# A graph attention layer: fetching 38 gathered rows a group by plain DMAs from two queues instead of 8 from one

## The chip, the cores and the metric

The kernel runs on one core of one Trainium2 chip. The metric is the device time of one execution in microseconds. Five engines work side by side: TensorE (PE, with its weight loads as PEld), VectorE (DVE), ScalarE (ACT), GpSimd (POOL) and SyncE (SP). Each has a queue of its own, worked off in order; semaphores tie them together.

## The reference

A graph has N = 12500 nodes and 212500 edges, sorted by destination. Node and edge features have 128 columns, in 8 heads of 16.

```python
Q = (x @ WQ).reshape(N, H, dh)
K = (x @ WK).reshape(N, H, dh)
V = (x @ WV).reshape(N, H, dh)
Eh = (edge_attr @ WE).reshape(-1, H, dh)
score = K[src] * Q[dst] / jnp.sqrt(jnp.float32(dh)) * Eh
score = jnp.exp(jnp.clip(score.sum(-1, keepdims=True), -5.0, 5.0))
msg = V[src] * score
wV = jax.ops.segment_sum(msg, dst, num_segments=N)
Z = jax.ops.segment_sum(score, dst, num_segments=N)
h = x + (wV / (Z + ATTN_EPS)).reshape(N, D)
# batch norm of h over the nodes, then layer norm of (x + that)
```

All data is float32. What this case is about is `K[src]` and `V[src]`: every edge needs the keys and values of its source node.

## The kernel before, in words

The edges stand in 1661 tiles of 128 edges, and up to 8 tiles make a group; there are 208 groups. First the kernel computes K and V of all nodes as one table `kvd` in DRAM, 1 KB a node (`table_rows`). For the first groups, while the table is still being made, it gathers x and projects it (`project_main`); from the ninth group on it gathers rows of the table into slots in SBUF, eight slots and one more later on.

The usual gather is one indirect DMA a tile, issued by POOL (line 223, `gather`): 128 rows of 1 KB by the node ids in `srcs`. The gathers of a group wait in a list, `queued`. In the main loop `pace` ties the first one of them to a matmul of the group (`add_x` or `q_mm`), and `issue` gives POOL the rest. A slot is free again when the message of its group has been computed.

Some tiles are gathered in another way. For each group in the list made by `row_plan`, the last of its eight tiles is not gathered by POOL. Its 128 rows are fetched one at a time by plain DMAs of 1 KB from SP (line 283, in `fetch_rows`), `SP_ROWS` = 8 of them in each group of the loop, into a tile `byrow` with two buffers. SP reads the byte offsets of the rows from `row_ids` into registers (line 276) and then issues a MOVE and a DMA a row. A tile so needs 16 groups of the loop to be filled, and it is used two groups after its last row (`ROW_LAG`). Twelve tiles are fetched so, 1536 rows. They count on semaphores of their own, `rows_in`; DVE waits for them (`rows_there`) before it uses such a tile, and it treats that tile apart from the other seven, in an instruction of its own, both for the product (line 630) and for the message (line 655).

The main loop is written out by hand, and each engine takes the instructions of a pass in that order. The parts that matter here are:

- SP loads `ea` for the group four ahead (line 508, three buffers), `relT` in fours (line 406) or singly (line 419), then fetches the rows.
- PE: `add_x` of the group three back (lines 696 and 697), `q_mm` of three ahead (563), `gather_sum` of the one before (670 and 671), `eh_mm` (584), `turn_back` (617), `qe_mm` (599).
- ACT: `x_out` of three back (701), `q_window` (525 and 532), `q_hi`, which copies Q out of PSUM (567), the two exponentials of this group in `clip_exp` (646 and 647), `sums_out` (676), the second copy of Q (572), `eh_out` (591).
- DVE: `products` (630), `q_lo` (575), `both_halves` (609), `scores` (637), the clip (645), `denom`, `recip` and `attn` (680, 683, 687), the one-hots (553, 543 to 546), `q_mid` (571), the message (655).

After the loop come the last groups, the two norms and the store of the output. A second way of computing it all, for inputs in another order, is not taken here.

Of the kernel before, what the change touches and what calls it, by code (L numbers as in the profile page):

```python
# [10 lines left out]
U8 = mybir.dt.uint8  # L11
I32 = mybir.dt.int32
AF = mybir.ActivationFunctionType
OP = mybir.AluOpType
AX = mybir.AxisListType
ET = mybir.EngineType

P = 128
# [4 lines left out]
U = 4  # L23
# [4 lines left out]
EARLY = 3  # L28
RUN = 64
ROWS = P  # L30
FIRST_ROW = 3
LATE = 8
ROW_LAG = 2
SP_ROWS = 8
WORDS = 4
RQ = 4
NSEM = 6
# [5 lines left out]
def plan(N, T):  # L43

    n, r = divmod(T - sum(LAST), U)
    sizes = [U] * n + [r] * (r > 0) + list(LAST)
    assert n > 1 and len(sizes) % 2 == 0
    starts = [sum(sizes[:g]) for g in range(len(sizes))]
    cuts = list(range(0, N - 64, CH)) + [N - 64, N]
    due = {}  # L50
    thr = [0.0] * len(sizes)
    for j, c in enumerate(cuts[1:]):
        need = (c + (64 if c < N - CH else 24)) * T
        g = next((g for g, t in enumerate(starts) if t * N >= need), None)
        if g is not None:
            due.setdefault(g, []).append(j)
            thr[g] = float(c)
    return sizes, starts, cuts, due, thr


def row_plan(sizes):


    full, n = sizes.count(U) // 2, SP_ROWS
    groups, end = [], P
    while FIRST_ROW + -(-end // n) - 1 + ROW_LAG < full:
        groups.append(max(NX, FIRST_ROW + -(-end // n) - 1 + ROW_LAG))
        end += P
    assert sorted(set(groups)) == groups
    return groups  # L70
# [7 lines left out]
def gnn_kernel(  # L78
# [19 lines left out]
    nc = tc.nc  # L98
    N, D = out.shape
    T = src.shape[1]  # L100
    NW = dstb.shape[1]
    usizes, ustarts, cuts, due, _ = plan(N, T)
    NG = NW // 2
    sizes = [usizes[2 * g] + usizes[2 * g + 1] for g in range(NG)]
# [5 lines left out]
    consts = ctx.enter_context(tc.tile_pool(name="consts", bufs=1))  # L110
# [50 lines left out]
    def load_rest():  # L161
        nc.scalar.dma_start(base_i, bass.AP(tensor=dstb.tensor, offset=dstb.offset, ap=[[0, P], [1, NW]]))
        nc.scalar.dma_start(rel_i[:, :cut], dst[:, :cut])
        load_row_ids()
        nc.scalar.dma_start(w_q, wq)
        nc.scalar.dma_start(w_e, we)
        nc.scalar.dma_start(srcs[:, nxg * G:cut], src[:, nxg * G:cut])

    def load_last():
        nc.scalar.dma_start(rel_i[:, cut:], dst[:, cut:])  # L170
        nc.scalar.dma_start(srcs[:, cut:], src[:, cut:])
        nc.scalar.dma_start(gb[:, 0:1], gamma)
        nc.scalar.dma_start(gb[:, 1:2], beta)
# [55 lines left out]
    def issue(n=0):  # L229
        while len(queued) > n:  # L230
            f, *a = queued.pop(0)
            f(*a)

    def pace(step):
        if queued:
            f, *a = queued.pop(0)
            tc.add_manual_dep(f(*a).ins, step.ins.name,
                              mybir.DependencyInfo(mybir.DependencyClass.Sync, mybir.DependencyReason.DATA),
                              reason="pace")
# [2 lines left out]

    by_row, fill = {}, {}
    row_loads = []
    n = SP_ROWS
    row_tiles = row_plan(usizes)
    tot = len(row_tiles) * P
    cols = -(-n // WORDS) * WORDS
    full_rows = tot // n
    blocks = -(-tot // (P * n))  # L250
    for q in range(0, full_rows, P):
        row_loads.append((0, q // P * cols, min(P, full_rows - q), n, q * n))
    if tot % n:
        row_loads.append((full_rows % P, full_rows // P * cols, 1, tot % n, full_rows * n))
    for q in range(-(-tot // n)):
        fill[FIRST_ROW + q] = q
    by_row.update({g: None for g in row_tiles})
    rows_in = [tc.alloc_semaphore(f"rows_in{i}") for i in range(NSEM)]
    row_ids = consts.tile([P, blocks * cols], I32, name="row_ids")
    nc.vector.memset(row_ids, 0)  # L260
    kvb = kvd.bitcast(U8).rearrange("n d -> (n d)")

# [1 line left out]
        return [(a, b - 1), (b - 1, b)] if g in by_row and b == G else [(a, b)]  # L264

    def load_row_ids():
        for p, c, m, w, at in row_loads:
            nc.scalar.dma_start(row_ids[p:p + m, c:c + w], bass.AP(
                tensor=rsrc.tensor, offset=rsrc.offset + at, ap=[[n, m], [1, w]]))

    def fetch_rows(g):
        if g not in fill:
            return
        q = fill[g]
        c = q // P * cols
        _, offs = nc.values_load_multi_w_load_instructions(
            row_ids[q % P:q % P + 1, c:c + cols], engines=(ET.SP,), min_val=0, max_val=(N - 1) * 8 * P,
            skip_runtime_bounds_check_because="node ids")
        for r, off in zip(range(q * n, min(q * n + n, tot)), offs):
            k = row_tiles[r // P]  # L280
            if r % P == 0:
                by_row[k] = rows.tile([P, 1, 2 * P], F32, name="byrow", bufs=2)
            d = nc.sync.dma_start(by_row[k][r % P:r % P + 1, 0, :].bitcast(U8), kvb[ds(off, 8 * P)].unsqueeze(0))
            d.then_inc(rows_in[r // P % NSEM], 16)
            tc.no_tile_sem_insts.add(d.ins.name)
            tc.add_to_no_dep_group(f"rows{k}", d.ins)
# [66 lines left out]
    def within(f, g):  # L353
        return f(g) if 0 <= g < NG else None
# [47 lines left out]
    def load_quad(q):  # L402
        t = late[0].tile([P, RQ, U * P], BF16, name="rbq", bufs=2)
        for h in (0, 1):
            at = ustarts[2 * RQ * q + h] * P
            nc.sync.dma_start(t[h * WN:(h + 1) * WN], bass.AP(
                tensor=relT.tensor, offset=relT.offset + at, ap=[[0, WN], [G * P, RQ], [1, U * P]]))
        for k in range(RQ):
            RB[RQ * q + k] = t[:, k, :]
# [191 lines left out]
    def ehqe(g):  # L601
        eh_mm(g)
        eh_out(g)
        qe_mm(g)
# [143 lines left out]
    for q in range(NQ):  # L748
# [13 lines left out]
        k = q - first_step  # L762
# [12 lines left out]
    q_mid(2)  # L775
    turn_back(0)
    ehqe(1)
    nc.vector.tensor_scalar(row_ids, row_ids, 8 * P, None, op0=OP.mult)
    within(load, 2)
    turned_onehot(2)  # L780
    load_rel(3)
# [10 lines left out]
    def bn_parts(a, b):  # L792
        for w in range(a, b):
            for j in due.get(w, []):
                bn_part(j)
                done.add(j)
# [22 lines left out]
    def within_checks(g):  # L819
        if g >= first_check and (g - first_check) % every == 0:  # L820
            check((g - first_check) // every)
# [6 lines left out]
    for g in range(NG - 2):  # L828
        within(load, g + 4)
        within(load_rel, g + 5)  # L830
        if (g + 6) % RQ == 0 and (g + 6) // RQ in quads:
            load_quad((g + 6) // RQ)
        fetch_rows(g)
        within(products, g)
        within(q_lo, g + 2)
        within(both_halves, g + 1)
        step = within(add_x, g - 3)
        step = within(q_mm, g + 3) or step
        if step is not None and queued and g >= LATE + 4:
            pace(step)  # L840
        issue()
        within(x_out, g - 3)
        within(q_window, g + 4)
        within(q_hi, g + 3)
        within(gather_sum, g - 1)
        within(eh_mm, g + 2)
        if g + 1 < nxg and g + 1 not in SLOT:
            for _ in project_main(g + 1):
                pass
        within(turn_back, g + 1)  # L850
        within(scores, g)
        within(clip_exp, g)
        within(sums_out, g - 1)
        within(denom, g - 2)
        within(recip, g - 2)
        within(attn, g - 2)
        within(turned_onehot, g + 3)
        within(onehot, g)
        within(q_mid, g + 3)
        within(eh_out, g + 2)  # L860
        within(qe_mm, g + 2)
        within(message, g)
        if g == NG - 3:
            onehot(g + 1)
        if g == 2:
            load_last()
        for r in runs[1:]:
            if g == max(4, r[0] // 2 - 12):
                place(r)
        within_checks(g)  # L870
        while free and todo and not pending:
            load_x()
        bn_parts(2 * g - 5, 2 * g - 3)
        if g == NG - 5:
            assert done >= set(range(NPRE))
            norm_first()
        if g == LATE - 1:
            tps.close()
            late.append(tps.enter_context(tc.tile_pool(name="late", bufs=1)))
        if g == LATE - 2:  # L880
            free.append(NSLOT)
            load_kv()
    last = NG - 1
    g = last - 1
# [4 lines left out]
                           skip_runtime_bounds_check_because="a count")]  # L889
# [7 lines left out]
    step = add_x(g - 3)  # L897
# [53 lines left out]
    pairs = [[i] for i in range(min(2, NY))] + [list(range(i, min(i + 2, NY))) for i in range(2, NY - 1, 2)]  # L951
# [261 lines left out]
```

## Time and profile before

| | |
|---|---|
| time, median of 3 runs | 2605.09 us (2600.39 to 2608.06) |
| the profiled execution | 2606.08 us, its span 2604.3 us |
| busy, share of the span | PE 72%, PEld 49%, DVE 64%, ACT 26%, POOL 61% |
| granted TensorE clock, mean | 0.839 |
| gathers by POOL (line 223) | 1585, mean 950 ns |
| row DMAs by SP (line 283) | 1536 of 1.0 KB |
| traffic | 148 GB/s over the span |

A line of a group in the profile gives the source line, the engine, the operation, what it writes and reads, the count, the busy time, the mean of one, and the engine's idle time just before it with what ended it. In a timeline the columns are the start in us from the start of the span, the length in us, the engine, the line, the operation, what it writes and reads and how many instructions were merged, with the idle time before it in brackets. The names SPq and ACTq stand for instructions that the engine's queue handles itself, among them the issue of DMAs; they are not counted as busy time. In a table by windows, the columns are the stretch, its length, the busy time of the engine with the number of instructions, the granted clock, the share of the DMA engines and GB/s.

### The profile page before, as it was taken

The numbers are of one execution on the slowest core, as the hardware profiler recorded it, in microseconds if no ns is written. First come the engines' busy times: TensorE is split into PE (matmuls) and PEld (weight loads), VectorE is DVE, ScalarE is ACT, GpSimd is POOL, SyncE is SP. The second block draws the span as 40 slices with busy tenths as digits, with TensorE's granted clock in tenths as the row PEclk, the third lists the DMA queues.
The fourth block names the chain that finished last, engine by engine and source line by source line (L and its number), as shares of the span: only waits on it lengthen the run. The fifth ranks groups of instructions, "written<-read, shape, count | busy, mean of one in ns | idle before, by whom it ended". The sixth has DMA issues, their size and how long they took to land. (4 is left out here: it accounts for less than half of the span.)

```text
span 2604.3 us, 34575 instructions
## 1 busy us (share of the span) xinstructions
PE 1872.5 (72%) x9414; PEld 1273.5 (49%) x9414; DVE 1656.1 (64%) x3577; ACT 677.8 (26%) x2480; POOL 1594.7 (61%) x1685
## 2 busy tenths in 40 slices
PE   7657677777777676777767767767776776677687
PEld 5435444444445454445545444445544454444456
DVE  3335666666666766666666666666666666666687
ACT  2223222222222222222222222222222222222235
POOL 6633566666666666666666666666666666666624
PEclk8978888888888988878787878888888888787889
DMA  7733454545445454454544544545445454454454
GB/s 231 245 110 97 143 149 141 155 145 149 147 139 157 146 149 145 138 157 138 157 145 140 149 142 148 147 146 146 149 142 150 142 152 145 141 155 138 144 161 118
DMA packets 175393, 386.62 MB, mean 148 GB/s; under 512 B 37518, under 2 KB 91831, under 8 KB 175191
## 3 DMA queue, kind: packets, MB, share of 16 engines
q0 software_dynamic: 78128, 212.05, 28.4%
q1 hardware_dynamic: 92900, 169.50, 20.7%
q10 hardware_dynamic: 4163, 2.78, 0.4%
q8 instruction: 77, 1.26, 0.2%
q14 instruction: 125, 1.02, 0.1%
HBM read 364.57 MB, written 19.63 MB: 148 GB/s over the span
## 5 line engine op out<-in xcount | busy, mean ns | idle before, releaser
L223 POOL DMA_INDIRECT slot<-kvd,srcs x1585 | 1506.0, 950 | 893.5 <-issue 416.9
L671 PE MATMUL ps_a<-msg,oh 128*128 128x136 f32 (+1 forms) x3322 | 705.8, 368 | 58.2 <-ACT os L676 48.3
L671 PEld LDWEIGHTS ps_a<-msg,oh 128*128 128x128 f32 (+1 forms) x3322 | 582.6, 222 | 170.7 <-issue 109.1
L609 DVE TENSOR_TENSOR wt<-wt,ps_q 128x512 f32<-128x512 f32 x416 | 276.5, 685 | 504.1 <-remote 212.1
L696 PE MATMUL ps_m<-ident,at 128*128 128x128 f32 x412 | 123.2, 390 | 492.6 <-issue 192.3
L584 PE MATMUL ps_e<-ea,w_e 128*128 128x512 f32 x832 | 395.2, 595 | 5.5 <-issue 4.9
L701 ACT ACTIVATE hx<-ps_m 128x64 f32 x412 | 93.2, 226 | 1137.6 <-PE ps_e L584 345.7
L696 PEld LDWEIGHTS ps_m<-ident,at 128*128 128x128 f32 x412 | 80.5, 243 | 585.5 <-issue 242.1
L630 DVE TENSOR_TENSOR p<-slot,ps_t 128x512 f32<-128x512 f32 (+1 forms) x410 | 264.0, 677 | 135.7 <-remote 91.7
L617 PEld LDWEIGHTS ps_t<-ident,wt 128*128 128x128 f32 x1661 | 191.8, 141 | 207.1 <-issue 142.4
L617 PE MATMUL ps_t<-ident,wt 128*128 128x128 f32 x1661 | 244.5, 278 | 64.9 <-issue 38.8
L591 ACT ACTIVATE wt<-ps_e 128x512 f32<-128x512 f32 x416 | 231.0, 587 | 128.7 <-remote 40.1
L637 DVE TENSOR_REDUCE s<-p 128x64 f32<-128x1024 f32 (+1 forms) x209 | 252.2, 1207 | 0.1
L655 DVE TENSOR_TENSOR msg<-slot,ps_m 128x1024 f32<-128x1024 f32 (+2 forms) x209 | 246.8, 1183 | 0.4 <-ACT ps_m L646 0.3
L543 DVE TENSOR_TENSOR oh<-ps_m,rel_i 128x512 f32<-128x512 f32 x208 | 142.3, 684 | 143.0 <-ACT ps_m L646 135.7
L584 PEld LDWEIGHTS ps_e<-ea,w_e 128*128 128x128 f32 x832 | 146.0, 194 | 109.2 <-issue 105.4
L599 PE MATMUL ps_q<-ot,q 64*128 64x512 bf16 x1248 | 174.6, 384 | 6.7 <-issue 6.7
L572 ACT ACTIVATE q<-qr 128x128 bf16<-128x128 f32 x208 | 64.7, 311 | 300.9 <-DVE qr L571 178.2
L563 PE MATMUL ps_m<-w_q,xw 128*128 128x128 f32 x416 | 109.4, 355 | 8.8 <-issue 8.6
L697 PE MATMUL ps_m<-xw,ident 128*128 128x128 f32 x412 | 106.7, 350 | 3.1 <-issue 2.9
L563 PEld LDWEIGHTS ps_m<-w_q,xw 128*128 128x128 f32 x416 | 89.9, 266 | 12.3 <-issue 12.2
L670 PE MATMUL ps_a<-os,carry 64*1 64x136 f32 x414 | 94.6, 314 | 1.2 <-issue 1.2
(173 smaller groups left out, 1516.3 us busy)
## 6 DMA issues: line engine op xcount, KB each, us to landing
ea<-eaT SPq DMA_DIRECT2D x207, 512.0 KB
slot<-kvd,srcs POOLq DMA_INDIRECT x1585
byrow<-kvd SPq DMA_DIRECT2D x1536, 1.0 KB
rbq<-relT SPq DMA_DIRECT2D x94, 256.0 KB
kvd<-slot SPq DMA_DIRECT2D x12, 512.0 KB
kvd<-t SPq DMA_DIRECT2D x12, 512.0 KB
slot<-xT SPq DMA_DIRECT2D x24, 256.0 KB
out<-o SPq DMA_DIRECT2D x23, 256.0 KB
```

The source lines that it names most:

```text
L223: return nc.gpsimd.indirect_dma_start(out=out, out_offset=None, in_=table, in_offset=bass.IndirectOffsetOnAxis(ap=srcs[:, e:e + 1], axis=0))
L563: return nc.tensor.matmul(PQ[g], XW[g], w_q, start=True, stop=True)
L584: nc.tensor.matmul(eh, w_e, EA[g][:, a:b, :].rearrange("p a b -> p (a b)"), start=True, stop=True)
L591: nc.scalar.activation(t[:, :(b - a) * P], EH[g][h], AF.Copy)
L599: nc.tensor.matmul(QE[g][h], Q3[g][r, k, :], OT[g][r, :(b - a) * P], start=(k == 0), stop=(k == 2))
L609: nc.vector.tensor_tensor(t, t, QE[g][h], op=OP.mult)
L617: nc.tensor.transpose(ps[:, j, :], WT[g][h][:, j * P:(j + 1) * P], ident)
L630: step = nc.vector.tensor_tensor(PR[g][:, c:d, :], KV[g](c, d, 0), PW[g][i][:, c - a:d - a, :], op=OP.mult)
L637: nc.vector.tensor_reduce(SS[g][:, a:b, :], PR[g][:, a:b, :].rearrange("p t (h d) -> p t h d", d=DH), axis=AX.X, op=OP.add)
L655: step = nc.vector.tensor_tensor(MSG[g][:, a:b, :P].rearrange("p t (h d) -> p t h d", d=DH), KV[g](a, b, P).rearrange("p t (h d) -> p t h ...
L671: nc.tensor.matmul(AGG[g][WN if j >= n else 0:], OH[g][j], MSG[g][:, j, :], start=(j == 0), stop=(j == n - 1))
L696: nc.tensor.matmul(ps, AT[g], ident, start=True, stop=False)
```

## The change

Each group of the loop now fetches 38 rows instead of 8: SP the first 21, at the same place as before, and ACT the other 17, between its copy of Q (`q_hi`) and the exponentials. Each engine loads its own offsets from `row_ids` first, 24 words on SP and 20 on ACT. A tile is full after 3.4 groups instead of 16, so the plan has 59 tiles fetched by rows instead of 12, and 7552 rows instead of 1536. The first group that fetches rows is 6 instead of 3, the last is 204. `row_ids` holds two groups a partition, and it is loaded by four DMAs of ACT in the pass of group 2 (`load_last`) instead of two at the start (`load_rest`); the multiplication that turns ids into byte offsets moves from before the loop to the pass of group 4.

```diff
-FIRST_ROW = 3
+FIRST_ROW = 6
-SP_ROWS = 8
+SP_ROWS = 21
+ACT_ROWS = 17
...
-    full, n = sizes.count(U) // 2, SP_ROWS
+    full, n = sizes.count(U) // 2, SP_ROWS + ACT_ROWS
...
     def load_rest():
...
-        load_row_ids()
...
     def load_last():
+        load_row_ids()
...
+    pairs = tot // (2 * n)
+    row_loads.append((0, 0, [[2 * n, pairs], [n, 2], [1, SP_ROWS]], 0, sp_step))
+    row_loads.append((0, act_at, [[2 * n, pairs], [n, 2], [1, ACT_ROWS]], SP_ROWS, act_step))
...
+    def offsets(q, et):
+        c, w, m = (0, sp_step, SP_ROWS) if et == ET.SP else (act_at, act_step, ACT_ROWS)
+        _, offs = nc.values_load_multi_w_load_instructions(
+            row_ids[q // 2:q // 2 + 1, c + q % 2 * w:c + (q % 2 + 1) * w], engines=(et,), min_val=0,
+            max_val=(N - 1) * 8 * P, skip_runtime_bounds_check_because="node ids")
+        return offs[:m]
+
+    def fetch_rows(g, et, a, b):
         if g not in fill:
             return
+        at = fill[g] * n
+        b = min(b, tot - at)
+        if b <= a:
+            return
+        eng = {ET.SP: nc.sync, ET.Activation: nc.scalar}[et]
+        for r, off in zip(range(at + a, at + b), offsets(fill[g], et)):
             k = row_tiles[r // P]
             if r % P == 0:
                 by_row[k] = rows.tile([P, 1, 2 * P], F32, name="byrow", bufs=2)
-            d = nc.sync.dma_start(by_row[k][r % P:r % P + 1, 0, :].bitcast(U8), kvb[ds(off, 8 * P)].unsqueeze(0))
+            d = eng.dma_start(by_row[k][r % P:r % P + 1, 0, :].bitcast(U8), kvb[ds(off, 8 * P)].unsqueeze(0))
...
-    nc.vector.tensor_scalar(row_ids, row_ids, 8 * P, None, op0=OP.mult)
...
-        fetch_rows(g)
+        fetch_rows(g, ET.SP, 0, SP_ROWS)
         within(products, g)
...
         within(q_hi, g + 3)
+        fetch_rows(g, ET.Activation, SP_ROWS, SP_ROWS + ACT_ROWS)
         within(gather_sum, g - 1)
...
             load_last()
+        if g == 4:
+            nc.vector.tensor_scalar(row_ids, row_ids, 8 * P, None, op0=OP.mult)
```

More of the change, by code (lines that the diff above doesn't have):

```diff
@@ L244, in gnn_kernel @@
     row_loads = []
-    n = SP_ROWS
+    n = SP_ROWS + ACT_ROWS
     row_tiles = row_plan(usizes)
     tot = len(row_tiles) * P
[L248 to L254, printed above, removed]
+    sp_step = -(-SP_ROWS // WORDS) * WORDS
+    act_at = 2 * sp_step
+    act_step = -(-ACT_ROWS // WORDS) * WORDS
+    pairs = tot // (2 * n)
+    assert pairs < P
+    row_loads.append((0, 0, [[2 * n, pairs], [n, 2], [1, SP_ROWS]], 0, sp_step))
+    row_loads.append((0, act_at, [[2 * n, pairs], [n, 2], [1, ACT_ROWS]], SP_ROWS, act_step))
+    for k in (0, 1):
+        left = tot - 2 * n * pairs - k * n
+        at = (2 * pairs + k) * n
+        for c, a, m in ((k * sp_step, 0, SP_ROWS), (act_at + k * act_step, SP_ROWS, ACT_ROWS)):
+            m = min(m, left - a)
+            if m > 0:
+                row_loads.append((pairs, c, [[1, 1], [1, 1], [1, m]], at + a, m))
     for q in range(-(-tot // n)):
         fill[FIRST_ROW + q] = q
+    cols = act_at + 2 * act_step
     by_row.update({g: None for g in row_tiles})
     rows_in = [tc.alloc_semaphore(f"rows_in{i}") for i in range(NSEM)]
-    row_ids = consts.tile([P, blocks * cols], I32, name="row_ids")
+    row_ids = consts.tile([P, cols], I32, name="row_ids")
     nc.vector.memset(row_ids, 0)
@@ L266, in load_row_ids @@
     def load_row_ids():
[L267 to L271, printed above, removed]
+        for p, c, ap, at, step in row_loads:
+            m, k, w = (d[1] for d in ap)
+            nc.scalar.dma_start(
+                row_ids[p:p + m, c:c + k * step].rearrange("p (k w) -> p k w", w=step)[:, :, :w],
+                bass.AP(tensor=rsrc.tensor, offset=rsrc.offset + at, ap=ap))
+    def offsets(q, et):
[5 more added lines that the diff above has]
+    def fetch_rows(g, et, a, b):
         if g not in fill:
             return
[L274 to L279, printed above, removed]
+        at = fill[g] * n
[4 more added lines that the diff above has]
+        for r, off in zip(range(at + a, at + b), offsets(fill[g], et)):
             k = row_tiles[r // P]
```

## The prediction

> **What bounds the kernel now.** I read the page's engine shares first, then the two windows over the long middle part, then the timeline of one group, then the timeline of a group at the end, where POOL has nothing left to gather.
>
> ```profile
> PE 1872.5 (72%) x9414; PEld 1273.5 (49%) x9414; DVE 1656.1 (64%) x3577; ACT 677.8 (26%) x2480; POOL 1594.7 (61%) x1685
> ...
> L223 POOL DMA_INDIRECT slot<-kvd,srcs x1585 | 1506.0, 950 | 893.5 <-issue 416.9
> ...
> L701 ACT ACTIVATE hx<-ps_m 128x64 f32 x412 | 93.2, 226 | 1137.6 <-PE ps_e L584 345.7
> ```
>
> No engine is full. ACT looks free (26%), and 1137.6 us of its waiting stands before one line, `x_out` (L701): 5.5 us a group over 208 groups. That is the time the change wants to use. The windows give the pace, for the scores' reduction (L637, one a group) and for the gathers (L223):
>
> ```profile
> 400.00:2400.00 2000.00, 207.46 (x171) 0.83 0.50 147
> ...
> 400.00:2400.00 2000.00, 1288.44 (x1358) 0.83 0.50 147
> ```
>
> So a group takes 2000/171 = 11.70 us and has 1358/171 = 7.94 gathers. Now one group, with instructions of every engine in order of time:
>
> ```profile
> 1210.97 0.95 POOL L223 DMA_INDIRECT slot<-kvd,srcs  x1 [2.00 <-PE ps_t L617]
> 1211.15 0.82 PE L599 MATMUL ps_q<-ot,q 64*128 64x512 bf16 x6
> 1211.64 0.36 SPq L508 DMA_DIRECT2D ea<-eaT  x1
> 1212.90 6.68 SPq L283 DMA_DIRECT2D byrow<-kvd  x8
> 1213.76 1.21 DVE L655 TENSOR_TENSOR msg<-slot,ps_m 128x1024 f32<-128x1024 f32 x1
> 1215.68 0.63 PE L697 MATMUL ps_m<-xw,ident 128*128 128x128 f32 x2
> 1219.73 0.95 POOL L223 DMA_INDIRECT slot<-kvd,srcs  x1 [0.30 <-issue]
> 1221.82 1.28 DVE L609 TENSOR_TENSOR wt<-wt,ps_q 128x512 f32<-128x512 f32 x2 [4.86 <-PE ps_a L671]
> 1222.61 0.48 ACT L701 ACTIVATE hx<-ps_m 128x64 f32 x2 [5.93 <-PE ps_e L584]
> 1222.79 0.95 POOL L223 DMA_INDIRECT slot<-kvd,srcs  x1 [2.12 <-PE ps_e L584]
> 1223.40 0.36 SPq L508 DMA_DIRECT2D ea<-eaT  x1
> 1223.43 0.26 ACT L567 ACTIVATE q<-ps_m 128x128 bf16<-128x128 f32 x1
> ```
>
> POOL issues a set of eight gathers, the first at 1210.97 and the eighth at 1219.73: one in 8.76/7 = 1.25 us. Then it waits 2.12 us for PE before the next set. While the set runs, what PE has finished reaches the others late: `ps_q` (L599) is done at 1211.97, and DVE's L609, which reads it, starts at 1221.82; L697 is done at 1216.31, and `x_out` (L701) starts at 1222.61. Both start just after the set has ended (1220.68). So the group is a set of gathers plus the hand-over after it: 7.94 x 1.25 = 9.9 us, plus 1.8. SP feels the same stretch: its eight row issues take 6.68 us there. Where POOL is done, the compute loop by itself looks like this:
>
> ```profile
> 2505.15 1.21 DVE L655 TENSOR_TENSOR msg<-slot,ps_m 128x1024 f32<-128x1024 f32 x1
> ...
> 2507.50 0.48 ACT L701 ACTIVATE hx<-ps_m 128x64 f32 x2 [0.95 <-PE ps_m L563]
> ...
> 2508.32 0.26 ACT L567 ACTIVATE q<-ps_m 128x128 bf16<-128x128 f32 x1
> ...
> 2510.41 0.23 ACT L646 ACTIVATE ps_m<-s 128x64 f32<-128x64 f32 x1 [1.82 <-DVE rz L680]
> ...
> 2511.28 0.68 DVE L543 TENSOR_TENSOR oh<-ps_m,rel_i 128x512 f32<-128x512 f32 x1
> ...
> 2512.66 1.21 DVE L655 TENSOR_TENSOR msg<-slot,ps_m 128x1024 f32<-128x1024 f32 x1
> ```
>
> Message to message is 7.5 us. The order matters for the change: message ends (2506.36), 1.14 us later `x_out` starts, then the windows of x, then Q's copy (L567, ends 2508.58), then the exponentials (L646), then the one-hot (L543), 2.59 us from its start to the end of the next message. Between Q's copy and the exponentials ACT has 1.8 us, not 5.5: the long wait stands ahead of `x_out`, the new issues stand behind it.
>
> **The change part by part.** *Gathers taken off POOL.* The plan has 59 tiles fetched by rows instead of 12, so 47 gathers of 1.25 us go: 59 us, if POOL's set still sets the pace. A set is then 8 - 59/199 = 7.70 gathers over the 199 groups that fetch rows (6 to 204).
>
> *Rows on SP and ACT.* The prices:
>
> ```profile
> 181.57 2.56 SPq L283 DMA_DIRECT2D byrow<-kvd  x8
> 198.39 2.86 SPq L283 DMA_DIRECT2D byrow<-kvd  x8
> ...
> 196.75 0.95 POOL L223 DMA_INDIRECT slot<-kvd,srcs  x1 [21.31 <-PE ps_t L340]
> ...
> 1200.25 1.24 SPq L406 DMA_DIRECT2D rbq<-relT  x2
> 1202.63 7.96 SPq L283 DMA_DIRECT2D byrow<-kvd  x8
> ...
> 1225.01 5.71 SPq L283 DMA_DIRECT2D byrow<-kvd  x8
> ...
> L283 SPq DMA_DIRECT2D byrow<-kvd x1536: 2/228/1395, 157.3 to 2428.4; - x192
> ...
> L276 SPq TENSOR_LOAD <-row_ids x192: 3/734/992, 156.2 to 2420.8; - x192
> ...
> L525 ACTq TENSOR_LOAD <-base_i x104: 303/308/577, 50.0 to 2515.3; - x104
> ```
>
> A row costs 2.56/8 = 0.32 us with POOL idle (21.31 us before 196.75) and 6.68/8 = 0.84 us beside a set, the middle one of three bursts in a row (7.96, 6.68, 5.71). No row DMA of ACT is in the trace; I give it SP's two prices. ACT's load of 20 words is not there either: flat it is 0.31 us (its four-word load), by SP's eight words 20/8 x 0.734 = 1.84; I take ACT's own rate, 5 x 0.308 = 1.54. The Trainium skill ("DMA: Bandwidth & Descriptors", Latency and other measured facts) gives such a load a floor of about 600 ns; ACT's 308 ns is under it, so the row decides. With 0.6 us in place of 1.54 the forecast below would be some 190 us lower.
>
> Now ACT's loop with the rows in it, from the start of `x_out` (X, 1222.61 in the group above; the set starts 0.18 later). Q's copy ends at X+1.08, the load at X+2.62. Eight rows at the price beside a set bring it to X+9.30; the set, 7.70 gathers long, ends at 0.18 + 7.70 x 1.25 - 0.30 = X+9.51. The other nine at 0.32 end at X+12.18. The scores are long there by then, as the message before and PE's products were not held. Then the exponential 0.23, one-hot to message 2.59, and 1.14 to the next `x_out`: X+16.1. That is 4.4 us over 11.70, and 199 groups make 876 us. Since POOL's set ends 6 us before the next begins, the 59 us are worth nothing here.
>
> *SP's part.* From its load of `ea` at X+0.8: 0.36, a load of 24 words (0.73 flat, 3 x 0.734 = 2.2 taken), `relT` 1.24/4 = 0.3 (L406, every fourth group), seven rows at 0.84 up to the set's end, 14 at 0.32 after it: done at X+14.0, so SP needs 13.2 us a group. Under 16.1 it stays hidden. Behind a row on SP wait `ea` for four groups on and `relT`; both are used two groups later. Behind ACT's rows stand the exponentials, the sums' copy, Q's second copy and `eh_out`, which is why ACT's price counts in full and SP's does not.
>
> *Waits.* The first row of a tile waits for the message that used the buffer two tiles before. By the plan that is one or two groups earlier; ACT fetches behind that message and does not wait, SP may stand up to half a group, once in 3.4 groups. At 16.1 us its 2.9 us of room a group covers that; without it, up to 1 us a group or 200 us.
>
> *DVE.* 47 more groups split product and message:
>
> ```profile
> L655 DVE TENSOR_TENSOR msg<-slot,ps_m 128x1024 f32<-128x1024 f32 x189 | 229.2, 1212 | 0.0
> ...
> L655 DVE TENSOR_TENSOR msg<-slot,ps_m 128x896 f32<-128x896 f32 x12 | 12.9, 1079 | 0.0
> ...
> L655 DVE TENSOR_TENSOR msg<-byrow,ps_m 128x128 f32<-128x128 f32 x12 | 3.4, 281 | 0.0
> ```
>
> The message grows by 1079 + 281 - 1212 = 0.15 us, in the loop: 47 x 0.15 = 7 us. The product's split lies beside PE.
>
> *Ids.* Two loads go from the start of ACT's queue, four come in the third group, and the multiplication moves to the fifth.
>
> ```profile
> 10.73 1.26 ACTq L268 DMA_DIRECT2D row_ids<-rsrc  x2
> ```
>
> That is -1.3 us at the start, beside the table's DMAs, and some 2.5 us once, where POOL and SP run ahead of ACT; I count nothing, between -1 and +3.
>
> *Sum.* 876 + 7 = 883 us on the profiled execution's own 2606.1 (span 2604.3, 1.8 around it; the median shown is 1 us less): **3489 us**.
>
> **The rivals.** *The rows hide (faster).* The loop is 1.08 + 0.23 + 2.59 + 1.14 = 5.04 plus ACT's burst; with a flat load (0.31) and 17 x 0.32 it is 10.8, under POOL's 7.70 x 1.25 + 1.8 = 11.4, and SP's 21 x 0.32 fit too. Then the 59 us come through: 2547 us. It decides below (11.4 - 5.04 - 0.31)/17 = 0.36 us a row. For it: the burst at 198.39 ran at 2.86 for eight although gathers had begun. Against it: the three bursts from 1202 to 1231 take two to three times as long.
>
> *SP becomes the bound.* ACT's rows cost 0.32 throughout (with the load of 1.54 its loop is 12.0), SP's as now: 13.2 us, 1.5 x 199 = 299 us, with DVE's 7: 2912. If SP's rows are cheap as well, ACT's 12.0 remains: 60 + 7 us, 2673, the low end of this case.
>
> *One gate for both queues.* If the two engines' issues go one after the other, about eight of the 38 rows go out beside the set, and ACT's last comes some 26 rows later. At the 228 ns that one issue holds SP, that is 5.9 us after X+9.5; with 3.96 to the next `x_out` a group is 19.4 us, 4145 in all. The Trainium skill ("Perfetto Trace Analysis", DMA Instruction — HWDGE) says that the sequencers issuing such DMAs share one descriptor generator, locked by one at a time; no run here shows two engines issuing rows at once, so this stays a rival.
>
> *The slow price throughout.* If rows cost 0.84 also after the set, ACT's burst ends at X+16.9: 20.8 us a group, 4424.
>
> That the change does not do what it says is out: a tile fetched by rows is a gather less in the queue that POOL is given.
>
> **How the numbers follow.** Forecast 0.33 (3489); SP the bound 0.28 (2673 to 2912); one gate 0.18 (4145); slow price 0.07 (4424). Together slower: 0.86. The rows hide: 0.11. Gain and loss cancel within 0.3%, about what a measurement here can tell: 0.03. The range takes in all slower cases, 2670 to 4430, and leaves out 0.14 below it and little above.
>
> **What would show it.** Right: ACT's byrow issues between L567's and L646's counterparts, some 11 us long, groups of about 16 us in the middle windows, POOL waiting 6 us between sets instead of 2. SP's burst shorter than the group. Wrong: ACT's burst under 6 us and POOL's gap still 2 us (rows hide), no wait of SP before its `ea` load (SP the bound), SP's and ACT's issues taking turns with both slower (one gate). It is wrong as a whole if a group stays under 11.7 us.

## The result, and the profile after

The changed kernel takes 3403.51 us (median of 4 runs, 3401.38 to 3411.59), the kernel before 2606.57 us beside it (2600.39 to 2609.4): 1.3067 times as long, 95% interval 1.3034 to 1.31. The forecast was 3489 us. The profiled execution took 3404.92 us, its span is 3403.1 us, its mean granted clock 0.747 (0.839 before). Chips differ here, which matters below: in two of the five series of runs `before` takes 2606 and 2608 us (whether on one chip or on two is not on record), in the other three, on three other chips, 2129 to 2135 us. So every kernel is compared with `before` in its own series. In what follows the first two series stand for a slower kind of chip and the other three for a quicker kind.

The profile page of the changed kernel, shares and groups:

```profile
PE 1971.7 (58%) x9414; PEld 1407.6 (41%) x9414; DVE 1665.0 (49%) x3671; ACT 667.1 (20%) x2480; POOL 1546.9 (45%) x1638
...
L224 POOL DMA_INDIRECT slot<-kvd,srcs x1538 | 1458.2, 948 | 1717.0 <-PE ps_m L581 1179.4
...
L664 ACT ACTIVATE ps_m<-s 128x64 f32<-128x64 f32 (+1 forms) x209 | 47.7, 228 | 1902.2 <-issue 1892.3
...
L719 ACT ACTIVATE hx<-ps_m 128x64 f32 x412 | 93.1, 226 | 373.5 <-PE ps_m L581 304.1
...
byrow<-kvd SPq DMA_DIRECT2D x4179, 1.0 KB
byrow<-kvd ACTq DMA_DIRECT2D x3373, 1.0 KB
```

ACT's wait has moved. Ahead of `x_out` (now L719) it fell from 1137.6 to 373.5 us; ahead of the first exponential (L664) stand 1902.2 us, 1892.3 of them ended by "issue", that is by ACT's own queue and by no other engine. POOL has 47 gathers less and is busy for 48 us less, but it waits more. Its view of waits, with total, number and longest:

```profile
ACT ps_m L664 <- issue: 1892.3, 197, 11.6
...
POOL slot L224 <- PE ps_m L581: 1179.4, 184, 8.7
```

ACT stands 1892.3/197 = 9.6 us a group ahead of the exponentials, and POOL 1179.4/184 = 6.4 us ahead of a set. The pace, by the scores' reduction (L655) in a window, and then one group in the timeline:

```profile
400.00:3200.00 2800.00, 215.52 (x177) 0.73 0.37 109
```

```profile
1606.42 0.48 ACT L719 ACTIVATE hx<-ps_m 128x64 f32 x2 [1.66 <-PE ps_m L581]
1606.61 0.95 POOL L224 DMA_INDIRECT slot<-kvd,srcs  x1 [4.04 <-PE ps_m L581]
...
1607.63 0.26 ACT L585 ACTIVATE q<-ps_m 128x128 bf16<-128x128 f32 x1
...
1608.33 0.20 DVE L663 TENSOR_SCALAR s<-s 128x64 f32<-128x64 f32 x1
...
1608.87 8.73 ACTq L301 DMA_DIRECT2D byrow<-kvd  x17
...
1617.70 0.23 ACT L664 ACTIVATE ps_m<-s 128x64 f32<-128x64 f32 x1 [9.81 <-issue]
...
1617.96 0.69 DVE L561 TENSOR_TENSOR oh<-ps_m,rel_i 128x512 f32<-128x512 f32 x1 [8.19 <-ACT ps_m L664]
...
1619.36 1.21 DVE L673 TENSOR_TENSOR msg<-slot,ps_m 128x1024 f32<-128x1024 f32 x1
...
1620.71 0.77 PE L714 MATMUL ps_m<-ident,at 128*128 128x128 f32 x2 [6.85 <-DVE msg L673]
...
1621.70 0.64 PE L581 MATMUL ps_m<-w_q,xw 128*128 128x128 f32 x2
...
1622.42 0.48 ACT L719 ACTIVATE hx<-ps_m 128x64 f32 x2 [1.66 <-PE ps_m L581]
1622.61 0.96 POOL L224 DMA_INDIRECT slot<-kvd,srcs  x1 [7.53 <-PE ps_m L581]
```

A group takes 2800/177 = 15.82 us. The clipped scores are ready at 1608.53 (L663), and the exponentials that read them start at 1617.70, when ACT's 17 row issues are out. Everything behind that waits in turn: DVE's one-hot 8.19 us, PE 6.85 us, POOL 7.53 us.

### The profile page after: what moved, and what is told of

Same layout as the page of the kernel before. It is cut to its first block, busy times and chain, and to the rows that moved or that the text cites. A ratio compares the mean times of both kernels' runs of the same rounds, so it can differ in the third digit from the quotient of the medians.

```text
span 3403.1 us, 46969 instructions
## 1 busy us (share of the span) xinstructions
PE 1971.7 (58%) x9414; PEld 1407.6 (41%) x9414; DVE 1665.0 (49%) x3671; ACT 667.1 (20%) x2480; POOL 1546.9 (45%) x1638
## 3 DMA queue, kind: packets, MB, share of 16 engines
q0 software_dynamic: 75872, 205.89, 20.8%
## 5 line engine op out<-in xcount | busy, mean ns | idle before, releaser
L224 POOL DMA_INDIRECT slot<-kvd,srcs x1538 | 1458.2, 948 | 1717.0 <-PE ps_m L581 1179.4
L714 PE MATMUL ps_m<-ident,at 128*128 128x128 f32 x412 | 154.3, 477 | 1287.5 <-DVE msg L673 861.4
L689 PE MATMUL ps_a<-msg,oh 128*128 128x136 f32 (+1 forms) x3322 | 785.8, 400 | 14.1 <-ACT os L694 11.9
L689 PEld LDWEIGHTS ps_a<-msg,oh 128*128 128x128 f32 (+1 forms) x3322 | 663.3, 250 | 130.5 <-issue 114.8
L714 PEld LDWEIGHTS ps_m<-ident,at 128*128 128x128 f32 x412 | 101.8, 307 | 1379.2 <-ACT wt L609 1325.8
L664 ACT ACTIVATE ps_m<-s 128x64 f32<-128x64 f32 (+1 forms) x209 | 47.7, 228 | 1902.2 <-issue 1892.3
L602 PE MATMUL ps_e<-ea,w_e 128*128 128x512 f32 x832 | 390.9, 592 | 0.7 <-ACT wt L609 0.7
L655 DVE TENSOR_REDUCE s<-p 128x64 f32<-128x1024 f32 (+1 forms) x209 | 253.0, 1210 | 0.1
L673 DVE TENSOR_TENSOR msg<-slot,ps_m 128x1024 f32<-128x1024 f32 (+3 forms) x209 | 240.6, 1153 | 0.4 <-ACT ps_m L664 0.3
L635 PE MATMUL ps_t<-ident,wt 128*128 128x128 f32 x1661 | 217.7, 273 | 8.8 <-ACT t L342 4.9
L602 PEld LDWEIGHTS ps_e<-ea,w_e 128*128 128x128 f32 x832 | 144.2, 192 | 100.4 <-issue 98.5
L719 ACT ACTIVATE hx<-ps_m 128x64 f32 x412 | 93.1, 226 | 373.5 <-PE ps_m L581 304.1
L715 PE MATMUL ps_m<-xw,ident 128*128 128x128 f32 x412 | 128.7, 415 | 0.0
L581 PEld LDWEIGHTS ps_m<-w_q,xw 128*128 128x128 f32 x416 | 111.6, 327 | 7.3 <-issue 7.2
```

Of the source, the lines that this page charges most:

```text
L224: return nc.gpsimd.indirect_dma_start(out=out, out_offset=None, in_=table, in_offset=bass.IndirectOffsetOnAxis(ap=srcs[:, e:e + 1], axis=0))
L581: return nc.tensor.matmul(PQ[g], XW[g], w_q, start=True, stop=True)
L602: nc.tensor.matmul(eh, w_e, EA[g][:, a:b, :].rearrange("p a b -> p (a b)"), start=True, stop=True)
L635: nc.tensor.transpose(ps[:, j, :], WT[g][h][:, j * P:(j + 1) * P], ident)
L655: nc.vector.tensor_reduce(SS[g][:, a:b, :], PR[g][:, a:b, :].rearrange("p t (h d) -> p t h d", d=DH), axis=AX.X, op=OP.add)
L673: step = nc.vector.tensor_tensor(MSG[g][:, a:b, :P].rearrange("p t (h d) -> p t h d", d=DH), KV[g](a, b, P).rearrange("p t (h d) -> p t h ...
```

## The experiments

**Theory and rivals.** The theory: ACT's burst lies whole in the chain from Q's copy to the exponentials, and that chain is the group; SP's rows and POOL's gathers lie beside it. Against it stand: SP's 21 rows are the bound; the two queues hinder each other; the burst costs the same wherever it lies; the slow price of rows beside POOL's gathers makes most of the loss. The expectations of the first four runs were written for a chip like the first; they ran on one where `before` takes 2131.39 us (8 runs, 2127.45 to 2133.31). So their figures in us are off as such, and what counts is which kernel loses.

**SP's rows alone.**

```diff
-ACT_ROWS = 17
+ACT_ROWS = 0
```

> SP alone fetches 21 rows a group, ACT none (32 tiles by rows). If ACT's burst ahead of the exponentials is what makes the group 15.8 us, the group falls back to 11.7 to 13.2 us (SP's own burst, 7 to 11 us, with its load and ea): 2580 to 2910 us. If the number of rows or SP's queue sets the pace, it stays near 15 us: 3200 to 3400 us.

Measured: 2109.51 us, ratio 0.9905 (0.9888 to 0.9921). Twice more on other chips of the quicker kind it came out the same, at 0.989 (0.9873 to 0.9906) and 0.9903 (0.9883 to 0.9924):

> The kernel of the first run once more (21 rows a group, all by SP, nothing on ScalarE), for a chip on which the kernel before takes about 2606 us. Theory (there a row costs 0.73 us on SP beside GpSimd's gathers, so SP itself becomes the bound, and ScalarE's load in the run with the load alone was innocent): ratio 1.15 as in that run. Rival (that run's 1.15 came from ScalarE's load): below 1.05. On a chip where before takes about 2131 us: 0.99 again, which tells nothing new.

> 21 rows a group by SP, nothing on ScalarE, a third time. Where before takes about 2606 us: by the theory that SP's rows at 0.73 us make SP the bound, ratio 1.15, as with ScalarE's load added; by the rival that ScalarE's load made that 1.15, below 1.05. Where before takes about 2131 us: 0.99 as twice before.

**ACT's rows alone.**

```diff
-SP_ROWS = 21
+SP_ROWS = 0
```

> ACT alone fetches 17 rows a group at the same place, SP none (26 tiles by rows). If ACT's burst sets the group: 14 to 16 us a group, 3050 to 3400 us; near the upper end if ACT's slow rows come from POOL's gathers, near 3050 if they come from SP issuing rows at the same time. If SP is the bound: 11.7 us a group or less, under 2620 us.

Measured: 2781.12 us, ratio 1.3022 (1.296 to 1.3083). Nearly the whole loss stands with ACT's rows (650 of the 684 us that the changed kernel loses on a chip of this kind, as measured below), although this kernel has only 26 tiles fetched by rows. The views of waits of the two, SP alone first:

```profile
POOL slot L224 <- issue: 442.6, 1451, 0.3
```

```profile
ACT ps_m L666 <- issue: 1355.6, 195, 7.5
```

With SP alone, 1451 of POOL's 1565 gathers wait for nothing but the 0.3 us between two issues: POOL works without a gap, and the 20 tiles more that SP takes off it are a gain. SP's own queue is full as well: its `ea` issues follow every 9.0 to 9.5 us (1002.57, 1011.55, 1020.51, 1029.97), about the group's 9.49 (158 groups in 1500 us), and between 400 and 1900 us it never waits longer than 0.7 us. With ACT alone, its queue holds the exponentials for 1355.6/195 = 7.0 us a group.

**Another place, and fewer rows.** The burst ahead of `x_out`, where the profile of before had ACT's long wait; and 9 rows instead of 17 at the place of the change.

```diff
-        fetch_rows(g, ET.Activation, SP_ROWS, SP_ROWS + ACT_ROWS)
...
+        fetch_rows(g, ET.Activation, SP_ROWS, SP_ROWS + ACT_ROWS)
         within(x_out, g - 3)
```

> All 38 rows, ACT's 17 moved ahead of x_out, where ACT waited 1137 us in the kernel before. If the burst is in the loop wherever it stands between eh_out and the exponentials, only the 1.1 us from message to x_out is now beside it: about 14.7 us a group, 3180 us. If the place was the mistake and that wait can hide the burst: 11.4 to 12 us a group, 2550 to 2650 us.

```diff
-ACT_ROWS = 17
+ACT_ROWS = 9
```

> 21 rows by SP and 9 by ACT (46 tiles by rows). If the group is 5 us plus ACT's burst, eight rows less at 0.32 to 0.84 and a load 8 words shorter (0.6) take 3.2 to 7.3 us off: 12 to 12.6 us a group at most before POOL or SP take over, 2660 to 2800 us. If rows in sum set the pace (30 of 38): 12.5 us above nothing, in proportion 15.8 x 30/38, again 12.5; if SP is the bound: 15.8 us, 3400 us.

Measured: ahead of `x_out` 2352.42 us, ratio 1.101 (1.0959 to 1.1062); with 9 rows 2120.9 us, 0.9956 (0.994 to 0.9972). The same 17 rows so cost a third as much (221 us, where the changed kernel loses 684 on this kind of chip, below) at a place where part of them is covered. Neither expectation for that place was met: 3180 us would be a ratio of 1.22 and 2550 to 2650 us one of about 1.0, and 1.10 lies between. One group of the kernel with the burst moved:

```profile
1009.85 1.06 ACT L609 ACTIVATE wt<-ps_e 128x512 f32<-128x512 f32 x2
...
1011.22 5.75 ACTq L301 DMA_DIRECT2D byrow<-kvd  x17
1011.93 0.63 PE L581 MATMUL ps_m<-w_q,xw 128*128 128x128 f32 x2
...
1017.13 0.48 ACT L719 ACTIVATE hx<-ps_m 128x64 f32 x2 [6.22 <-PE ps_a L689]
...
1018.63 0.23 ACT L664 ACTIVATE ps_m<-s 128x64 f32<-128x64 f32 x1
```

PE has `x_out`'s input at 1012.56; ACT takes it up at 1017.13, 4.6 us late. The rest of load and burst is covered by the message and by PE. With 9 rows the burst is about 3 us, and the kernel makes 158 groups in 1500 us, as many as with SP alone. ACT's loop has not fallen clear of the others there:

```profile
ACT ps_m L666 <- issue: 518.0, 134, 4.3
```

ACT's own queue still holds 134 of the exponentials, POOL has no gaps, and SP waits 1.1 us at the longest between 400 and 1900 us, so three limits lie close together. The 14 gathers less than with SP alone, 17 us, bring nothing: the kernel takes 11 us longer.

**The four on the slower kind of chip.** Beside the changed kernel once more: the burst behind the exponentials, ACT's load without any rows (and SP's 21), and the burst in three parts. `before` took 2608.22 us here (7 runs, 2601.55 to 2610.21).

> The changed kernel itself, unchanged, beside the other kernels of this call. Where the kernel before takes about 2131 us in this call (GpSimd's gathers at 1.25 us without gaps, a row at 0.32 us): ScalarE's loop 5.0 + load 1.3 + 17 rows 5.8 = 12.1 to 12.7 us a group, about 2780 us, ratio about 1.30. Where it takes about 2606 us: as measured at first, 3403 us, ratio 1.31. Rival (the price lies in the slow rows alone): on a chip without the slow stretch the ratio would be below 1.1.

Measured: 3411.93 us, ratio 1.3073 (1.3042 to 1.3104).

```diff
         within(clip_exp, g)
+        fetch_rows(g, ET.Activation, SP_ROWS, SP_ROWS + ACT_ROWS)
         within(sums_out, g - 1)
```

> 38 rows a group as in the changed kernel, ScalarE's 17 moved from behind Q's copy to directly behind the two exponentials. Theory (the burst costs whatever of it the loop cannot cover, and the only cover is the 2.6 us of one-hot and message on VectorE): behind it ScalarE still has the sums' copy, Q's second part and the two edge copies, which TensorE needs before the next x_out, so the loop is about 10.9 us a group, ratio about 1.14, between the changed kernel's 1.30 and the 1.10 of the place ahead of x_out. Rival (any place behind the exponentials is free, as message and the next x_out need 3.7 us anyhow): 9.2 us a group, ratio about 1.0.

```diff
-ACT_ROWS = 17
+ACT_ROWS = 0
...
-        fetch_rows(g, ET.Activation, SP_ROWS, SP_ROWS + ACT_ROWS)
+        if g in fill:
+            offsets(fill[g], ET.Activation)
```

> SP fetches 21 rows a group as in the run with SP alone; ScalarE only loads 20 offsets a group into its registers at the changed kernel's place and fetches nothing with them. Theory: the load holds ScalarE for 1.3 us, the loop is 5.0 + 1.3 = 6.3 us, far below GpSimd's set, so the time is that of SP alone, ratio 0.99. Rival (the load is what hurts, since the chain to the exponentials is tight): 199 groups at 1.3 us, +259 us, ratio about 1.11.

```diff
+        fetch_rows(g, ET.Activation, SP_ROWS, SP_ROWS + 6)
         within(gather_sum, g - 1)
...
         within(sums_out, g - 1)
+        fetch_rows(g, ET.Activation, SP_ROWS + 6, SP_ROWS + 12)
...
         within(message, g)
+        fetch_rows(g, ET.Activation, SP_ROWS + 12, SP_ROWS + ACT_ROWS)
```

> 38 rows a group, ScalarE's 17 in three parts: 6 behind Q's copy (with the load), 6 behind the copy of the sums, 5 behind the edge copies. Theory (each part is paid less what ScalarE stood idle at that place: none, 1.2 and 1.0 us): 5.0 + 1.3 + 2.0 + 0.8 + 0.7 = 9.8 us a group, ratio about 1.05. Rival (17 rows cost the same wherever they lie): as the changed kernel, 1.30.

Measured: behind the exponentials 3118.32 us, 1.1958 (1.1913 to 1.2004); the load alone 3007.6 us, 1.1524 (1.1497 to 1.1551); in three parts 3263.73 us, 1.2519 (1.2493 to 1.2545). All three are far above what I expected. The load alone was to cost nothing, and by its rival some 259 us for itself; neither is what happens. SP's own queue in the timeline of the load alone shows why:

```profile
1577.01 0.18 SPq L528 DMA_DIRECT2D ea<-eaT  x1
1579.00 9.60 SPq L303 DMA_DIRECT2D byrow<-kvd  x21
1588.71 0.36 SPq L528 DMA_DIRECT2D ea<-eaT  x1
1590.88 10.91 SPq L303 DMA_DIRECT2D byrow<-kvd  x21
1601.81 0.69 SPq L528 DMA_DIRECT2D ea<-eaT  x1
1603.99 13.48 SPq L303 DMA_DIRECT2D byrow<-kvd  x21
1617.66 0.26 SPq L528 DMA_DIRECT2D ea<-eaT  x1
```

Each `ea` follows within 0.2 us on the burst before it, each burst follows on `ea` as soon as its offsets are loaded (1.5 to 1.8 us later): over these 40 us SP waits for nobody. And the others wait for SP: in the waits of this kernel, PE for `ea` and DVE for a tile of rows.

```profile
PE ps_e L604 <- DMA ea<-eaT: 501.6, 107, 10.3
...
DVE p L650 <- DVEq L310: 240.4, 19, 18.4
```

So on this kind of chip SP becomes the bound as soon as ACT's burst is out of the way, at 2000/145 = 13.79 us a group (145 groups in the window 400:2400). The kernels with the burst moved or split have SP's 21 rows too, and so could hardly come under that; DVE waits in them for tiles of rows, 419.8 us over 34 waits behind the exponentials and 666.2 us over 48 in three parts. SP's queue waits in both for at most 1.0 us at a time between 400 and 2400 us, so it is the bound there too, at 2000/140 = 14.29 and 2000/134 = 14.93 us a group. That is 0.5 and 1.1 us above the 13.79 without rows on ACT: whether the two queues hinder each other by that much no run tells. What three parts cost by themselves cannot be read from a kernel bound like this. SP alone, without ACT's load, ran only on chips of the quicker kind, so that SP is at 13.8 us there without the load too is read from this trace and was not measured.

**Without POOL's gathers.** From group 24 on the gathers of kv are left out; the messages use stale rows.

```diff
-            for j in range(sizes[g] - (g in by_row)):
+            for j in range(G if g < 24 else 0):
```

> The changed kernel with GpSimd's gathers of kv left out from group 24 on (the messages then use stale rows); all 38 rows a group stay as they are. Theory (the slow rows come from GpSimd's gathers, and ScalarE's loop is the bound with or without them): every row at 0.32 us, group 5.0 + 1.4 + 5.7 = 12.1 us, so 3403 - 185 x 3.7 = about 2720 us on any chip. Rival 1 (the slow rows are the chip's own and have nothing to do with GpSimd): still 15.8 us a group, about 3400 us where before takes 2606. Rival 2 (GpSimd's set is the bound after all): well below 2400 us.

**The changed kernel on a quicker chip.**

> The changed kernel itself, beside the kernel before. Theory (ScalarE's loop is the bound, and it depends on the chip only through the price of a row): where before takes about 2131 us, 5.0 + 1.4 + 5.7 = 12.1 to 12.6 us a group as without the gathers, 2760 to 2830 us, ratio 1.29 to 1.33; where before takes about 2606 us, 3400 to 3415 us, ratio 1.31. Rival (the slow rows make up most of the loss): below 1.15 on the quicker chip.

Measured: without gathers 2807.81 us where `before` takes 2135.02 (2130.24 to 2136.81); the changed kernel 2812.83 us (2811.28 to 2817.74) where it takes 2129.14 (2126.61 to 2134.01), ratio 1.3215 (1.3185 to 1.3244). The windows, by the scores' reduction, without the gathers first:

```profile
400.00:2400.00 2000.00, 186.08 (x154) 0.79 0.19 55
```

```profile
400.00:2400.00 2000.00, 187.40 (x154) 0.79 0.46 132
```

Both have 154 groups in 2000 us, 12.99 us a group. POOL's gathers are worth nothing at all in the changed kernel on such a chip (the second rival is out), and the loop that sets the pace is ACT's. The group is longer than the 12.1 us expected, and the time without gathers 88 us above the 2720. Whether the slow rows of the slower kind would go with the gathers, the first rival, this run could not tell, as it ran on a quicker chip.

```profile
1599.53 5.84 ACTq L301 DMA_DIRECT2D byrow<-kvd  x17
...
1605.48 0.23 ACT L664 ACTIVATE ps_m<-s 128x64 f32<-128x64 f32 x1 [7.12 <-issue]
...
1610.20 0.48 ACT L719 ACTIVATE hx<-ps_m 128x64 f32 x2 [1.66 <-PE ps_m L581]
1610.38 0.94 POOL L224 DMA_INDIRECT slot<-kvd,srcs  x1 [4.49 <-PE ps_m L581]
...
1611.41 0.26 ACT L585 ACTIVATE q<-ps_m 128x128 bf16<-128x128 f32 x1
```

Here the rows cost 5.84/17 = 0.34 us even beside POOL's set. The rival that the slow rows make up most of the loss is out: without them the loss is still 684 us.

The best of all is SP's 21 rows with nothing on ACT: 1% quicker than `before`, on three chips of the quicker kind. By the 13.8 us a group above it should lose on the slower kind; it did not run there.

## Why the prediction was right

**The mechanism.** "The long wait stands ahead of `x_out`, the new issues stand behind it": that is what the waits show, 1892.3 us ahead of L664 with no other engine to blame. On the quicker kind of chip, the two runs that each leave out one engine's rows put the loss on ACT's, and the burst ahead of `x_out` shows that the place, and not the rows as such, sets the price. On the slower kind, where the forecast was made, the kernels without ACT's burst at that place run into SP's limit, so that there the waits alone show it.

**The size.** Forecast 16.1 us a group, measured 15.82. Over 199 groups, 15.82 - 11.70 makes 820 us; the two profiled executions lie 798.8 us apart (3404.92 - 2606.08), the forecast had 883, with DVE's 7; the 21 us between 820 and 798.8 are not explained. That the group came within 0.3 us is in part luck, as three terms moved against each other, 1.5 us too much in the first and 1.15 us too little in the other two:

- From Q's copy to the exponentials: forecast 11.10 us (load 1.54, rows 9.56), measured 9.6 by the waits. The lines of the load's instruction in the changed kernel, with shortest, median and longest in ns:

```profile
L284 SPq TENSOR_LOAD <-row_ids x199: 651/1672/2015, 210.2 to 3330.1; - x199
L284 ACTq TENSOR_LOAD <-row_ids x199: 1238/1436/1481, 218.1 to 3330.5; - x199
```

  ACT's took 1.44 us, so that its length was forecast well; the Trainium skill ("DMA: Bandwidth & Descriptors", Latency and other measured facts) gives 0.6 us as a floor, which the four-word loads before the change, 0.31 us, are under. But it does not stand whole behind Q's copy: in the group above the copy ends at 1607.89 and the first row follows 0.98 us later, so about 0.5 us of the load lies beside the copy. The other mis-sized part is the rows: all 17 took 8.73 us there, not 9.56. The price of a slow row was right and the stretch was not. The first eight rows take 2.77 us (0.35 each), although POOL's set has run since 1606.61; the next six, up to 1616.65, take 0.83 us each; the last three 0.32. So the slow stretch begins 5.0 us after the set's start and ends 1.6 us after the set's last gather (1615.08), and it holds six rows and not eight.
- From the exponentials to the next `x_out`: forecast 0.23 + 2.59 + 1.14 = 3.96 us, measured 4.72 (1617.70 to 1622.42). The 1.14 came from a stretch where PE had been busy. The same step in the run with 9 rows:

```profile
1002.47 0.23 ACT L666 ACTIVATE ps_m<-s 128x64 f32<-128x64 f32 x1 [4.20 <-issue]
...
1005.48 0.46 PE L716 MATMUL ps_m<-ident,at 128*128 128x128 f32 x2 [1.18 <-DVE msg L675]
...
1006.00 0.39 PE L583 MATMUL ps_m<-w_q,xw 128*128 128x128 f32 x2
...
1006.48 0.48 ACT L721 ACTIVATE hx<-ps_m 128x64 f32 x2 [0.95 <-PE ps_m L583]
```

  There it is 4.01 us, and PE's three pairs take 0.91 us (1005.48 to 1006.39). In the changed kernel they take 1.63 us (1620.71 to 1622.34), after PE had stood idle for 6.85 us. The forecast did not count that a longer group makes the idle engine's own part longer.
- From the start of `x_out` to the end of Q's copy: forecast 1.08, in the group shown 1.47 (1606.42 to 1607.89), in the next 1.20 (1622.42 to 1623.62).

**POOL.** "The 59 us are worth nothing" and "6 us between sets instead of 2": 6.4 us. Where the burst is not in the way they are worth something: SP alone takes 20 tiles off, 25 us at 1.25 us, and gains 22.

**SP.** "Needs 13.2 us, hidden under 16.1": it needs 13.8 where it is the bound, and in the changed kernel it stays hidden: it waits 344.0 us for PE (L602) before its `ea` loads there. On the quicker kind it needs about 9.5.

**The rivals.** *The rows hide* counted a flat load of 0.31 us and the short way to `x_out`. On the quicker kind of chip rows do cost 0.34 us, so that its condition of 0.36 us a row was met, and the loop is 12.99 us all the same: the load takes 1.44 (about 1.0 of it behind Q's copy), not 0.31, and the step after the exponentials 4.72. *SP becomes the bound* was a true second limit, waiting right behind ACT's; its 2912 compares with 3007.6 for the load alone. *One gate for both queues* (the Trainium skill, "Perfetto Trace Analysis", DMA Instruction — HWDGE) does not decide here. The timeline of the kernel with the burst behind the exponentials, on the slower kind of chip:

```profile
1603.06 6.70 SPq L301 DMA_DIRECT2D byrow<-kvd  x21
1603.54 6.00 ACTq L301 DMA_DIRECT2D byrow<-kvd  x17
...
1607.63 0.94 POOL L224 DMA_INDIRECT slot<-kvd,srcs  x1 [11.80 <-PE ps_m L581]
...
1613.57 16.54 SPq L301 DMA_DIRECT2D byrow<-kvd  x21
```

Both queues issue at the same time, SP at 6.70/21 = 0.32 us a row and ACT at 6.00/17 = 0.35, while POOL stands idle for most of it. If they share a generator, it leaves each about the rate it has alone there; its 19.4 us a group are out by the 15.82. *The slow price throughout* (20.8 us a group) is out by the 15.82.

**What was wrong.** The prediction took the slow price of rows beside POOL's set for a property of the kernel. It is not there in the three series of runs on quicker chips: the forecast in us holds for the slower kind alone. That the ratio is 1.31 on the one kind and 1.32 on the other is chance, from two different sums: 4.1 us more on a group of 11.70 us there, about 3.5 us more on one of 9.5 us here (1500/158, with SP alone, which is near `before` in time).

## What to carry to other kernels

An engine that is busy for a quarter of the time is free only at the places where its waits stand: read which instruction the idle time precedes, and put new work ahead of that instruction, not behind it (here that cost a third as much, and not nothing). An instruction that issues a DMA holds its engine like any other (0.32 to 0.35 us a row here, up to 0.83 on the slower kind of chip, and 1.44 us for the offsets), and on an engine in the chain it counts in full beyond the slack of its place. Moving work off one engine pays only down to the next limit, and here a second one, SP, lay close behind; the best that was measured, a gain of 1% with SP alone, left the engine in the chain untouched.

## What the runs showed of the hardware

**Two kinds of chip.** The same `before` took 2606.57 and 2608.22 us in two series of runs and 2131.39, 2135.02 and 2129.14 us in three, on three other chips. On the slower kind, a burst of 21 rows takes 6.70 us where POOL stands idle or has just begun and up to 16.54 us beside its gathers (the rows under *One gate* above). On the quicker kind the same burst runs beside gathers that follow on each other without a gap:

```profile
1004.27 0.95 POOL L224 DMA_INDIRECT slot<-kvd,srcs  x1 [0.31 <-issue]
...
1004.74 6.70 SPq L303 DMA_DIRECT2D byrow<-kvd  x21
...
1005.52 0.94 POOL L224 DMA_INDIRECT slot<-kvd,srcs  x1 [0.30 <-issue]
```

(SP's rows alone.) A gather takes POOL 0.95 us on both. The mean traffic is 184 GB/s here and 148 in the profile of before. What differs between the chips stays open: no run tells it. That it is the chip at all is read from the five series; no chip is known to have come up twice.

**PE after a pause.** The three pairs of matmuls that `x_out` waits for take 0.91 us after 1.2 us of idle time and 1.63 us after 4.2 to 6.9 us of it, on both kinds of chip. The Trainium skill ("TensorE: Matmul & The Clock Gate", Part 1) says that PE's clock is halved after a window of about 3.4 us without work; these rows agree with that, and no run here moved the pause alone. Pauses in between went either way in the profile of before: the three pairs took 1.61 us after 2.98 us of idle time (from 1039.93) and 0.91 us after 3.50 us (from 1052.18), so no sharp limit can be read from these traces.
